# A four-layer graph network on one core: the instruction order as a stored table, and layer 0's tile turned through DRAM

## The chip, the core and the metric

The kernel runs on one core of a Trainium2 chip. The metric is device microseconds of one launch; the time before is the median of three runs. Engines go by their short names: PE (TensorE, the matrix engine), PEld (its weight loads), DVE (VectorE), ACT (ScalarE), POOL (GpSimd), SP (the queue that issues all the DMAs).

## What is computed

64 graphs of 256 nodes with 256 features go through four layers. Each is `x = x + layer(relu(layernorm(x)), adj)`:

```python
h = jnp.maximum(_layernorm(x, axis=-1), 0.0)
x = x + _L0_gnn_ref(h, adj, Wq, Wk, Wv, Wo, bo)   # masked attention, 8 heads of 32
h = jnp.maximum(_layernorm(x, axis=-1), 0.0)
x = x + _L1_gnn_ref(h, adj, W, a)                 # additive attention, softmax over axis 1, elu
h = jnp.maximum(_layernorm(x, axis=-1), 0.0)
x = x + _L2_gnn_ref(h, adj, weight, w_ih, w_hh, b_ih, b_hh)   # 3 rounds: A^T (h W_i), then a GRU cell
h = jnp.maximum(_layernorm(x, axis=-1), 0.0)
x = x + _L3_gnn_ref(h, adj, W, b, a)              # additive attention, 4 heads of 64
```

All of it is float32. In layer 0

```python
scores = jnp.where(adj > 0, q @ k.T / sqrt(32), -1e9)
w = softmax(scores)
out = (w @ v) @ Wo + bo
```

## The kernel before

**Tiling.** Two graphs make a pair; there are 32 pairs. A pair's x is one tile of 128 partitions by 1024 (four blocks of 128 nodes by 256 features). The loop over pairs at the end of the kernel does not issue anything: each step of each layer is given to `plan.add` with the engine or engines that may do it, its planned duration, what it reads and writes, and the buffers that it claims. The tile pool is by hand: `SLOTS` says how many buffers of each kind there are (22 of the large `w4`, 10 `part`, 6 `mask`, 8 banks of PSUM `ps`).

**Order.** `Plan.order` then places all 13630 steps one after the other. In before it is a list scheduler: of the steps whose inputs are placed and for which a buffer is free it takes the one that can begin first by its planned times. Ties are broken by a key: the pair's number times `PERIOD`, plus a number from `KEYS` for the stage (such as "0s", layer 0's scores) and the kind of engine, with a set of their own for the first pair ("<") and for the last two (">"). Where a step has two forms (`evict` at L380/L381 copies a PSUM bank out on ACT or on DVE; `either` goes to POOL or DVE) the scheduler chooses one. The buffer that a step gets is fixed there too. Each engine then executes its instructions strictly in the order so made, and SP issues all DMAs in its own. No time of the plan is measured; on the chip each engine waits for semaphores wherever its inputs are late.

**The start of a layer** is `norm_relu`. Statistics on DVE (L555, L557), the reciprocal root on POOL (L568, L569), then the scaled tile `xn` on ACT (L582) or DVE (L588). Matmuls need the features in partitions, so `xn` is turned. There are two ways. The one on PE: eight transposes of 128 by 128 into two PSUM banks (L627), and relu while copying out of PSUM on ACT or DVE (L639, L640). The other, `turn_rows`: DVE turns the 32 by 32 blocks of the tile (L731), one DMA writes the result to DRAM (L686) and four read it back with the blocks exchanged (L689); then relu goes from SBUF to SBUF. `by_dma` chooses: in before the second way is used for layer 2 (and for its state between its rounds, "2m", L718) in all pairs but the last. Layers 0 and 3 go by PE.

**Other lines of PE.** Layer 0: L786 q and k, L662 v, L807 scores (a mode that uses a quarter of the rows for each of four matmuls), L859 attention times v (a quarter of the columns), L874 the output product. Layer 1: L980, L994. Layer 2: L1064 messages, L1087 the GRU's gates. Layer 3: L1209, L1263 (half of the columns), and in the last pair alone L707, L1308. L1170 is layer 2's way back to rows in the last pair. L415, L437, L477 and L524 prepare weights once. Changing between full and partial use of the array is a mode switch.

**Other lines.** L697: DVE turns the blocks of attention weights, which then go through DRAM by L686 and L689 too. L755 adds mask and finds the minimum, L762 is exp with its sum, L839 divides a row on ACT or DVE, L1048/L1049 and L1099/L1097 are steps of layer 2 with a form on either engine, L1144 and L1184 are additions on DVE or POOL. L1117, L1135, L1150 and L1155 are the rest of the GRU on DVE.

Of the kernel before, what the change touches and what calls it, by code (L numbers as in the profile page):

```python
# [35 lines left out]
class Task:  # L36
    __slots__ = ("pair", "forms", "bufs", "rank", "stage", "mode", "before", "after", "waits", "begin", "end", "engine", "latency", "rest", "key", "index")


class Plan:  # L40

    HOP = {"PE": 0.22, "DVE": 0.15, "ACT": 0.17, "POOL": 0.2, "SP": 0.1}
    SAME = {"PE": 0.0, "DVE": 0.1, "ACT": 0.1, "POOL": 0.1, "SP": 0.0}  # L50

    SPARE, GRAIN = 2, 0.001
    SLOW, MARGIN = 1.4, 0
    BACK = {"DVE": 0.3, "POOL": 1.1}


    PERIOD = 2538  # L60


    KEYS = {
        ("io<", "SP"): -105537, ("w<", "SP"): 5780, ("w<", "on"): 21835, ("w<", "PE"): 92045, ("0n<", "on"): -17,
        ("0n<", "SP"): 6914, ("0n<", "PE"): -3050, ("0<", "on"): -27933, ("0<", "PE"): -18831,
        ("0s<", "PE"): -43638, ("0s<", "on"): 32209, ("0e<", "on"): 33228, ("0e<", "SP"): 79294,
        ("0c<", "PE"): -5710, ("0c<", "on"): 78141, ("1n<", "on"): -3936, ("1n<", "SP"): 18999, ("1<", "on"): 8087,
        ("1r<", "on"): -58751, ("1r<", "SP"): -50364, ("1e<", "on"): -20926, ("1c<", "PE"): -18939,
        ("1c<", "on"): -36902, ("2n<", "on"): -9735, ("2n<", "SP"): -46049, ("2<", "on"): 22518,
        ("2h<", "PE"): 10890, ("2h<", "on"): 963, ("2m<", "on"): -12912, ("2m<", "PE"): -339, ("2r<", "PE"): 6753,  # L70
        ("2r<", "on"): -6234, ("2z<", "PE"): 8380, ("2z<", "on"): -1814, ("2u<", "PE"): 8044, ("2u<", "on"): -10808,
        ("2b<", "on"): -14087, ("2b<", "SP"): 20724, ("3n<", "on"): -11783, ("3n<", "SP"): 82960,
        ("3n<", "PE"): -19591, ("3<", "on"): 17546, ("3<", "PE"): -92746, ("3r<", "on"): -497, ("3r<", "SP"): 37604,
        ("3e<", "on"): 40267, ("3e<", "SP"): 17882, ("3c<", "PE"): 7194, ("3c<", "on"): -53745,
        ("3b<", "on"): -23800, ("3b<", "SP"): -32005, ("out<", "SP"): -30439, ("io", "SP"): -97593,
        ("0n", "on"): -7813, ("0n", "SP"): 7384, ("0n", "PE"): -775, ("0", "on"): -21029, ("0", "PE"): -7985,
        ("0s", "PE"): -38312, ("0s", "on"): 31183, ("0e", "on"): 32073, ("0e", "SP"): 77616, ("0c", "PE"): 2974,
        ("0c", "on"): 57928, ("1n", "on"): -15346, ("1n", "SP"): 35194, ("1", "on"): 12385, ("1r", "on"): -77012,
        ("1r", "SP"): -49238, ("1e", "on"): -28359, ("1c", "PE"): -2261, ("1c", "on"): -48562, ("2n", "on"): -10735,
        ("2n", "SP"): -38216, ("2", "on"): 11427, ("2h", "PE"): 6520, ("2h", "on"): -16065, ("2m", "on"): -22340,  # L80
        ("2m", "PE"): 4183, ("2r", "PE"): 6841, ("2r", "on"): -20226, ("2z", "PE"): 8470, ("2z", "on"): 15796,
        ("2u", "PE"): 7640, ("2u", "on"): -22009, ("2b", "on"): -4038, ("2b", "SP"): 33111, ("3n", "on"): 144,
        ("3n", "SP"): 39097, ("3n", "PE"): -5812, ("3", "on"): 17370, ("3", "PE"): -71538, ("3r", "on"): 9250,
        ("3r", "SP"): 47648, ("3e", "on"): 7306, ("3e", "SP"): 29172, ("3c", "PE"): 14097, ("3c", "on"): -46777,
        ("3b", "on"): -25269, ("3b", "SP"): -31168, ("out", "SP"): -26306, ("io>", "SP"): -77815,
        ("0n>", "on"): -18200, ("0n>", "SP"): 5368, ("0n>", "PE"): -2327, ("0>", "on"): -9215, ("0>", "PE"): -23927,
        ("0s>", "PE"): -39218, ("0s>", "on"): 29982, ("0e>", "on"): 28489, ("0e>", "SP"): 110800,
        ("0c>", "PE"): 3058, ("0c>", "on"): 51808, ("1n>", "on"): -9527, ("1n>", "SP"): 16664, ("1>", "on"): -2988,
        ("1r>", "on"): -65640, ("1r>", "SP"): -57698, ("1e>", "on"): -21072, ("1c>", "PE"): -19804,
        ("1c>", "on"): -62098, ("2n>", "on"): -8753, ("2n>", "SP"): -47004, ("2>", "on"): 5930, ("2h>", "PE"): 1570,  # L90
        ("2h>", "on"): 2104, ("2m>", "on"): -12945, ("2m>", "PE"): 3645, ("2r>", "PE"): 7126, ("2r>", "on"): -31799,
        ("2z>", "PE"): 8512, ("2z>", "on"): -12839, ("2u>", "PE"): 7096, ("2u>", "on"): -20477, ("2b>", "on"): 2677,
        ("2b>", "SP"): 20159, ("3n>", "on"): -5070, ("3n>", "SP"): 60459, ("3n>", "PE"): -8408, ("3>", "on"): 8430,
        ("3>", "PE"): -69282, ("3r>", "on"): -4245, ("3r>", "SP"): 18290, ("3e>", "on"): 10463,
        ("3e>", "SP"): 23776, ("3c>", "PE"): 16211, ("3c>", "on"): -38642, ("3b>", "on"): -42787,
        ("3b>", "SP"): -42858, ("out>", "SP"): -18723, ("2n>", "PE"): 5512, ("2b>", "PE"): -10868,
        ("3e>", "PE"): -146212, ("3b>", "PE"): -24496,
    }


    SWITCH = 0.19
    HOLD = (0.00, 0.00, 0.00)
    MODES = ("full", "rows", "columns", "halves")

    def __init__(self, slots, spare):
        self.slots, self.spare = slots, spare
        self.pairs = []
        self.stage, self.rank, self.place = "", None, ""
# [4 lines left out]
    def add(self, forms, reads=(), writes=(), latency=0.0, claims=(), mode="full"):  # L113

        t = Task()  # L120
        t.pair, t.forms = len(self.pairs) - 1, [forms] if isinstance(forms, tuple) else forms
        t.before, t.after, t.bufs, t.latency = set(), [], [], latency
        t.end = t.engine = None
        t.rank = (t.pair if self.rank is None else self.rank, len(self.pairs[-1]))
        t.stage, t.mode = self.stage + self.place, mode
# [25 lines left out]
    def data(self, t, engine):  # L151

        return max(
            (x.end + (self.HOP[x.engine] if x.engine != engine else self.SAME[x.engine]) for x in t.before), default=0.0
        )

    def order(self):

        every = [t for tasks in self.pairs for t in tasks]
        spares = dict(self.spare, w4=self.SPARE)  # L160
        for i, t in enumerate(every):
            t.index, t.waits = i, len(t.before)
            for x in t.before:
                x.after.append(t)
            for b in t.bufs:
                b.until, b.left = 0.0, 0
                if not b.tag:
                    b.slot = 0
        for t in every:
            engine = t.forms[0][0]  # L170
            kind = engine if engine in ("PE", "SP") else "on"
            t.key = t.rank[0] * self.PERIOD + t.rank[1] * 1e-4 + self.KEYS.get((t.stage, kind), self.KEYS.get((t.stage.strip("<>"), kind), 0.0))
        for t in every:
            for b in t.bufs:
                b.left += 1
        free, now = {}, "full"
        slots = {tag: [(0.0, i) for i in range(n)] for tag, n in self.slots.items()}
        out = []
        left = [len(tasks) for tasks in self.pairs]
        ready = [t for t in every if not t.waits]  # L180
        oldest = 0
        while ready:
            best, fit, tiled = None, [], dict.fromkeys(self.MODES, 0)
            for t in ready:
                start = 0.0
                new = [b.tag for b in t.bufs if b.slot is None]
                for tag in set(new):
                    n = new.count(tag)
                    have = slots[tag]
                    if len(have) < n + (spares.get(tag, 0) if t.pair != oldest else 0):  # L190
                        break
                    start = max(start, have[n - 1][0])
                else:
                    fit.append((t, start))
                    if t.mode != "full" and max(start, self.data(t, "PE")) <= free.get("PE", 0.0) + 0.3:
                        tiled[t.mode] += 1
            for t, start in fit:
                for form in t.forms:
                    engine, key = form[0], t.key
                    data = max(start, self.data(t, engine))  # L200
                    begin = max(data, free.get(engine, 0.0), free.get("port", 0.0) if len(form) > 3 else 0.0)
                    at = begin
                    if engine == "PE":
                        if t.mode != now:
                            hold = self.HOLD[self.MODES.index(t.mode) - 1] if t.mode != "full" else 0.0
                            if hold and tiled[t.mode] < 2:
                                at = max(at, data + hold)
                            begin = max(at, free.get("PE", 0.0) + self.SWITCH)
                        elif t.mode != "full":
                            key -= 1e6  # L210
# [1172 lines left out]
```

## Time and profile before

| | |
|---|---|
| median of 3 runs | 3517.14 us (3517.03 to 3518.95) |
| the profiled execution | 3519.16 us |
| its span in the trace | 3517.4 us |
| granted clock of PE, mean | 0.993 |
| DMA | 720.92 MB, 64.9% of 16 engines' span in the main queue |

The rows of groups read: line, engine, operation, written tile <- read tiles, shapes, count | busy time in us, mean ns of one | idle time of the engine just before them, and what ended it.

```profile
L1087 PE MATMUL ps<-w,whhT 128*128 128x512 f32 x2304 | 1067.7, 593 | 1.5 <-DMA w<-turn 1.5
L627 PE MATMUL ps<-ident,w 128*128 128x128 f32 x520 | 70.9, 279 | 14.1 <-ACT w L582 14.0
L639 ACT ACTIVATE w<-ps 128x512 f32<-128x512 f32 x126 | 68.6, 599 | 84.6 <-PE ps L627 84.6
L731 DVE STREAM_TRANSPOSE w<-w 128x1024 f32<-128x1024 f32 x31 | 38.3, 1236 | 0.8 <-ACT w L582 0.8
L381 DVE COPY w<-ps 128x512 f32<-128x512 f32 x81 | 53.0, 682 | 11.7 <-PE ps L980 4.1 <-PE ps L1263 3.3 <-PE ps L1170 2.7
```

Mean durations of neighbours on one engine overlap, so a group's busy time is the union of its instructions' times. A float32 matmul of the program stands as two instructions in the trace, a transpose as one.

### The profile page before, as it was taken

The page shows a single profiled execution, that of the slowest core. Times are in us where ns is not written, and L with a number is a line of the kernel's source. Part 1 is how long each engine was busy: PE and PEld are TensorE (multiplying, and loading weights), DVE is VectorE, ACT ScalarE, POOL GpSimd, SP SyncE. Part 2 cuts the span into 40 slices and gives each one's busy share as a digit, 9 for nine tenths or more (in the row PEclk, how much of TensorE's full clock was granted, in tenths as well). Part 3 has the DMA queues.
Part 4 walks back from the last instruction along what each step waited for, and adds up shares of the span by engine and source line. Part 5 has one row for each costly group of instructions (what it writes and reads, how often), then busy time and mean ns, then how long its engine had stood idle before and what let it go on. Part 6 is the DMA issues. An engine that isn't in the chain of part 4 may idle for free.

```text
span 3517.4 us, 54023 instructions
## 1 busy us (share of the span) xinstructions
PE 3457.1 (98%) x15032; PEld 1944.5 (55%) x15032; DVE 2873.1 (82%) x8732; ACT 2674.8 (76%) x7097; POOL 347.9 (10%) x435
## 2 busy tenths in 40 slices
PE   9899999999999999999999999999999999999996
PEld 5455555555555555555555555555555555555553
DVE  6888987888988888978888878888878889887665
ACT  6776877877877877878877878878878778776545
POOL 2000110111001111001111001111001111001000
PEclk9999999999999999999999999999999999999998
DMA  6765677667667667667667666667666667666243
GB/s 195 216 190 179 213 225 222 204 213 231 211 203 220 211 204 239 205 205 219 212 203 234 207 209 218 210 208 234 204 210 215 211 215 232 202 217 191 96 138 126
DMA packets 573761, 720.92 MB, mean 205 GB/s; under 512 B 96532, under 2 KB 488724, under 8 KB 573460
## 3 DMA queue, kind: packets, MB, share of 16 engines
q1 hardware_dynamic: 573460, 717.46, 64.9%
q8 instruction: 121, 1.98, 0.2%
q14 instruction: 180, 1.47, 0.1%
HBM read 410.53 MB, written 298.34 MB: 202 GB/s over the span
## 4 chain that ended last, share of the span: by engine, by line
PE 90%; DVE 2%; ACT 1%; DMA 1%; issue 0%; SPq 0%; POOL 0%; DVEq 0%; ACTq 0%
PE ps L1087 54%; PE ps L1064 5%; PE ps L786 5%; PE ps L807 3%; PE ps L1209 3%; PE ps L1263 3%; PE ps L980 3%; PE ps L859 3%; PE ps L994 3%; PE ps L662 3%; PE ps L874 3%; PE ps L627 1%; DMA w<-turn 1%; DVE w L755 0%; ACT w L762 0%; DVE w L697 0%
## 5 line engine op out<-in xcount | busy, mean ns | idle before, releaser
L1087 PE MATMUL ps<-w,whhT 128*128 128x512 f32 x2304 | 1067.7, 593 | 1.5 <-DMA w<-turn 1.5
L1087 PE MATMUL ps<-w,giT 128*128 128x512 f32 x2304 | 1058.3, 592 | 0.7 <-ACT w L380 0.7
L762 ACT ACTIVATE w<-w,mx 128x256 f32<-128x256 f32 x1536 | 760.5, 504 | 7.5 <-DVE mx L755 7.4
L1087 PEld LDWEIGHTS ps<-w,giT 128*128 128x128 f32 x2304 | 436.8, 190 | 544.6 <-issue 527.9
L1087 PEld LDWEIGHTS ps<-w,whhT 128*128 128x128 f32 x2304 | 426.2, 190 | 467.5 <-issue 430.9
L380 ACT COPY w<-ps 128x512 f32<-128x512 f32 (+1 forms) x519 | 295.1, 580 | 290.7 <-PE ps L786 119.3
L697 DVE STREAM_TRANSPOSE w<-w 128x1024 f32<-128x1024 f32 x380 | 466.4, 1233 | 38.8 <-ACT w L839 28.2
L755 DVE CUSTOM_DVE_ANT_0 w<-ps,mask 128x256 f32<-128x256 f32 x1024 | 367.3, 416 | 21.0 <-PE ps L807 20.9
L839 ACT ACTIVATE w<-w,rz 128x256 f32<-128x256 f32 x782 | 341.9, 508 | 4.5 <-DVE rz L832 4.4
L762 ACT ACTIVATION_READ_ACCUMULATOR w<-w,mx 128x1 f32 x1536 | 301.2, 196 | 0.0
L1135 DVE TENSOR_TENSOR w<-ps,w 128x512 f32<-128x512 f32 x192 | 129.4, 674 | 209.1 <-PE ps L1087 208.5
L568 POOL TENSOR_SCALAR rs<-mv 128x4 f32<-128x4 f32 x129 | 32.5, 252 | 2703.1 <-DVE mv L557 2680.1
L582 ACT ACTIVATE w<-x,rs 128x256 f32<-128x256 f32 x492 | 257.4, 605 | 16.3 <-DVE rs L574 16.1
L1139 ACT ACTIVATE w<-w,bih_sb 128x512 f32<-128x512 f32 x192 | 138.4, 721 | 168.0 <-DVE w L1135 167.9
L1064 PE MATMUL ps<-part,part 128*128 128x256 f32 x1536 | 236.5, 303 | 5.3 <-DVE part L1022 4.3
L1240 ACT ACTIVATE w<-w,f 128x256 f32<-128x256 f32 x512 | 220.1, 498 | 5.5 <-DMA w<-row 5.4
L1112 ACT ACTIVATE w<-ps,brz 128x512 f32<-128x512 f32 x192 | 131.4, 685 | 121.8 <-PE ps L1087 121.7
L1064 PEld LDWEIGHTS ps<-part,part 128*128 128x128 f32 x1536 | 199.5, 190 | 41.2 <-issue 28.2
L755 DVE CUSTOM_DVE_ANT_0 w<-w,mask 128x256 f32<-128x256 f32 x512 | 195.4, 427 | 18.8 <-ACT w L1240 16.6
L1126 ACT ACTIVATE w<-ps,brz 128x512 f32<-128x512 f32 x192 | 131.8, 686 | 82.9 <-PE ps L1087 82.6
L555 DVE BATCH_NORM_STATS2 st<-x 128x6 f32<-128x256 f32 x512 | 188.8, 410 | 2.8 <-DMA x<-in_x_dram 2.3
L1117 DVE SCALAR_TENSOR_TENSOR w<-w,w 128x512 f32<-128x512 f32 x192 | 130.3, 679 | 60.5 <-ACT w L1112 58.0
(116 smaller groups left out, 4928.6 us busy)
## 6 DMA issues: line engine op xcount, KB each, us to landing
turn<-w SPq DMA_DIRECT2D x504, 512.0 KB
w<-turn SPq DMA_DIRECT2D x2016, 128.0 KB
w<-in_adj_dram SPq DMA_DIRECT2D x128, 512.0 KB
w<-row SPq DMA_DIRECT2D x64, 512.0 KB
x<-in_x_dram SPq DMA_DIRECT2D x64, 256.0 KB
out_dram<-x SPq DMA_DIRECT2D x64, 256.0 KB
turn<-w SPq DMA_DIRECT2D x62, 256.0 KB
w<-turn SPq DMA_DIRECT2D x248, 64.0 KB
```

The lines of the kernel that those rows point to most:

```text
L380: (A, act(n), lambda: nc.scalar.copy(dst(), src())),
L555: nc.vector.bn_stats(st()[:, t, :], tok(xt())[:, t, :])
L582: nc.scalar.activation(tok(xn())[:, t, :], tok(xt())[:, t, :], func, bias=rs()[:, 1, t : t + 1], scale=rs()[:, 0, t : t + 1])
L697: add((V, dve(T * N), lambda: nc.vector.transpose(blocks(), blocks())), writes=[e])
L755: nc.vector.tensor_tensor_reduce(row, src, mask, scale, 3.0e38, ALU.add, ALU.min, mn)
L762: nc.scalar.activation(row(e, r), row(e, r), AF.Exp, bias=mn()[:, r : r + 1], scale=-1.0, accum_out=zs()[:, z0(r) : z0(r) + 1])
L786: mm(ps(), w[:, k, o * P : (o + 1) * P], wide(hT, k), start=k == 0, stop=k == 1)
L839: op(row, row, rz()[:, r : r + 1])
L1064: mm(ps()[:, o * N : (o + 1) * N], chunk_of(part(), h.mixed, c, o), tok(ams[g](), N)[:, c, :], start=i == 0 and c == 0, stop=i == 1 and c ...
L1087: mm(ps(), w[:, k, c0 : c0 + P], wide(src, k), start=n == 0, stop=n == 2 * len(terms) - 1)
L1139: (A, act(N2, 1), lambda o=o, hn=hn: nc.scalar.activation(at_o(hn, o), at_o(hn, o), AF.Tanh, bias=bih_sb[:, 4 + o : 5 + o])),
L1240: nc.scalar.activation(dst, src, AF.Prelu, bias=f()[:, t, D + h : D + h + 1], alpha=ALPHA)
```

## The change

`Plan.order` no longer chooses. A table `ORDER` (a compressed byte string) holds three bytes for each step: the low and the high byte of a signed difference, and the number of the form. `ranked` adds the differences up within a pair to a rank, and the steps are sorted by it; `order` walks the sorted list, asserts that a step's inputs have been placed, and hands out buffers as before, by its planned times. The keys, the spare counts of the buffers and the ranks of the weights are gone. `SLOTS` has 21 `w4`, 11 `part` and 7 `mask`. `TURNED` has "0" too, so that layer 0's tile takes `turn_rows` in all pairs but the last. Every computed value is the same. New lines stand 37 below those of before (34 in the last part of the file): L627 is L664.

```diff
-    SPARE, GRAIN = 2, 0.001
-    SLOW, MARGIN = 1.4, 0
-    BACK = {"DVE": 0.3, "POOL": 1.1}
-    PERIOD = 2538
-    KEYS = {
...
-    }
+    SLOW, SWITCH = 1.4, 0.19
+
+    ORDER = (
...
+    )
+    def ranked(self):
+
+        every = [t for tasks in self.pairs for t in tasks]
+        n = len(every)
+        raw = zlib.decompress(base64.b85decode(self.ORDER))
+        assert len(raw) == 3 * n
+        low, high, forms = raw[:n], raw[n : 2 * n], raw[2 * n :]
+        rank, pair = 0, None
+        for t, a, b, form in zip(every, low, high, forms):
+            step = a + 256 * b
+            rank = (rank if t.pair == pair else 0) + (step - 65536 if step > 32767 else step)
+            pair = t.pair
+            t.rank, t.form = rank, t.forms[form]
+        return sorted(every, key=lambda t: t.rank)
...
-        while ready:
-            best, fit, tiled = None, [], dict.fromkeys(self.MODES, 0)
...
+        for t in every:
+            engine, us, do = t.form[:3]
+            assert t.before <= done
+            begin = max(free.get(engine, 0.0), free.get("port", 0.0) if len(t.form) > 3 else 0.0)
+            for x in t.before:
+                begin = max(begin, x.end + (self.HOP[x.engine] if x.engine != engine else self.SAME[engine]))
             for b in t.bufs:
                 if b.slot is None:
-                    _, b.slot = slots[b.tag].pop(0)
+                    at, b.slot = slots[b.tag].pop(0)
+                    begin = max(begin, at)
...
-        "w4": (22, [P, T * D], FP, 2),
-        "part": (10, [P, N2], FR, 1),
+        "w4": (21, [P, T * D], FP),
+        "part": (11, [P, N2], FR),
...
-        "mask": (6, [P, T * N], BF, 1),
+        "mask": (7, [P, T * N], BF),
...
-    TURNED = ("2", "2m")
+    TURNED = ("0", "2", "2m",)
...
-            for plan.rank, weights in ((None, weights0), (RANKS[0], weights1), (RANKS[1], weights2), (RANKS[2], weights3)):
+            for weights in (weights0, weights1, weights2, weights3):
                 weights()
```

## The prediction

> **What bounds the kernel now.** I read the busy shares first, then a table of the engines over seven stretches of the span, then the waits of TensorE, then the queue of TensorE in order of time, and last the groups by line and shape.
>
> ```profile
> PE 3457.1 (98%) x15032; PEld 1944.5 (55%) x15032; DVE 2873.1 (82%) x8732; ACT 2674.8 (76%) x7097; POOL 347.9 (10%) x435
> ```
>
> TensorE is busy for 3457.1 of 3517.4 us, so it idles 60.3 us; VectorE and ScalarE have 644 and 843 us free. The stretches (busy time of PE, PEld, DVE, ACT, POOL, then granted clock, DMA share, GB/s) tell where the 60 us lie:
>
> ```profile
> 0.00:110.00 110.00, 100.88 (x518) 64.39 (x519) 76.38 (x273) 75.20 (x207) 24.55 (x32) 1.00 0.65 208
> 110.00:250.00 140.00, 120.91 (x616) 72.16 (x615) 119.68 (x398) 110.47 (x316) 6.53 (x9) 0.94 0.70 210
> 250.00:500.00 250.00, 248.75 (x1054) 134.72 (x1053) 218.73 (x644) 180.38 (x481) 25.62 (x30) 1.00 0.62 194
> 500.00:3000.00 2500.00, 2500.00 (x10913) 1406.04 (x10911) 2077.93 (x6352) 1979.69 (x5258) 243.26 (x309) 1.00 0.68 215
> 3000.00:3400.00 400.00, 399.04 (x1610) 220.08 (x1609) 312.20 (x871) 266.61 (x674) 37.63 (x44) 1.00 0.54 170
> 3400.00:3460.00 60.00, 57.49 (x194) 29.39 (x192) 36.80 (x91) 27.33 (x61) 5.66 (x6) 1.00 0.39 123
> 3460.00:3518.00 58.00, 30.07 (x136) 17.75 (x136) 31.41 (x108) 35.09 (x105) 4.64 (x6) 0.71 0.43 137
> ```
>
> Idle TensorE: 9.1 us at the start, 19.1 us between 110 and 250, 2.2 us from 250 to 3400, 30.4 us behind 3400. From 500 to 3000 it has none, and no wait of TensorE is listed there. A busy row of matmuls is not yet a full TensorE, since their ends are modelled, so I look at starts: the queue of TensorE, start and length, shows each group beginning when the one before has issued its last.
>
> ```profile
> 1499.79 1.50 PE L1209 MATMUL ps<-w3a,w 128*128 128x264 f32 x6
> 1501.12 1.04 PE L627 MATMUL ps<-ident,w 128*128 128x128 f32 x8
> 1502.00 1.88 PE L1087 MATMUL ps<-w,whhT 128*128 128x512 f32 x4
> 1503.72 1.88 PE L1087 MATMUL ps<-w,giT 128*128 128x512 f32 x4
> 1505.43 3.60 PE L786 MATMUL ps<-w,wq_sb 128*128 128x512 f32 x8
> 1508.87 3.60 PE L786 MATMUL ps<-w,wk_sb 128*128 128x512 f32 x8
> ```
>
> Four matmuls of 512 columns take 1.72 us from start to start, every time: TensorE runs at its issue rate. The chain of waits repeats the same pieces every 106.02 us (one pair of graphs), and within such a period TensorE works 106.02 us, VectorE 88.20, ScalarE 84.22, GpSimd 10.22. So in the middle the only thing that shortens the kernel is fewer or cheaper instructions on TensorE; at the two ends it is fewer waits.
>
> **What the Trainium skill says.** "TensorE: Matmul & The Clock Gate", Part 4: PE-mode transpose, gives about 275 ns for one in context. Here the duration agrees (273 ns), but eight go from 1501.12 to 1502.00, so in a full queue one costs 0.11 us; I use that. The same page, Part 1, says that an idle window halves the clock until TensorE has been busy again: the trace agrees, 0.94 granted between 110 and 250 and 0.71 behind 3460, the two stretches with long waits. "VectorE: DVE Perf Modes", The three transpose paths: VectorE turns 32x32 blocks only, which is why the blocks must then be moved by DMA; the trace has this form at L731, 1236 ns for 128x1024. "SBUF — State Buffer", SBUF: two separate sides: GpSimd and certain VectorE operations lock a shared port pair from each other; no row here separates such blocking.
>
> **The change part by part** (line numbers of before; the counts of after are from the instruction order of the two programs).
>
> *Transposes of layer 0.* L627 falls from 520 to 272: 31 pairs by 8 leave. 248 x 0.109 (0.88 over 8) = 27.0 us off TensorE, and all on the bounding queue except the first few pairs. With them go 62 PSUM banks' worth of turns. Layer 0's tile now goes VectorE transpose (31 more of L731), one DMA to DRAM, four DMAs back, relu out of SBUF. This path is longer: in before the four reads are issued about 2.9 us after the write, when they follow at once (37.15 to 40.07), and the reads land some us later. That costs nothing while the pair starts early enough, and six buffers of x let its input be loaded ahead. It is not free for pair 0, where nothing lies ahead; there TensorE now starts with weight work before the first L786: 40 transposes at 0.11 and 36 of L477's 48 matmuls at 0.32 (three quarters of 0.43), 16 us. From the first start of TensorE in before (7.8 us, when the scaled tile is there) the turned tile needs 1.24 + 2.9 + the reads, for which I take 4, + 0.6 = 9 us, so the 16 us hide it.
>
> *Mode switches.* Counting changes between full, row, column and half use of the array in TensorE's order gives 364 before and 326 after. From the queue, a block of 16 at L807 holds it for 1.08 us (1521.34 to 1522.42), one of 64 at L859 for 3.59 (1515.83 to 1519.42): 0.052 each and 0.24 per block, 0.12 a switch. 38 x 0.12 = 4.6 us; I take 4.
>
> *Forms moved between engines.* VectorE gets 87 more copies out of PSUM (L381, 0.65), 28 of L588 (0.36), 104 of L839 (0.31), 52 of L1099 (0.74), 31 of L731 (1.24), 35 relus out of SBUF (no row before; between L1049's 0.43 and L640's 0.65, I take 0.6), and some 40 smaller (0.55), and loses 51 of L1144 (0.69) to GpSimd and about 10 of L1184: 57+10+32+38+38+21+22-35-6 = 177, less overlaps of neighbours about 165 us. VectorE goes to 2873+165 = 3038, 87% of 3483; in the middle 88.2+5.3 = 93.5 of 105.1 us. ScalarE loses roughly 87x0.58+28x0.52+104x0.44+52x0.67+43x0.6+20x0.6 = 183, to 71%. GpSimd gains 51x1.29+12x0.74 = 75, to 12%. All lie beside TensorE, and cost nothing while VectorE stays under it. Without that cover each us of VectorE beyond TensorE's in a period costs 1 us by 28 periods.
>
> *DMA and SP.* 155 more issues (31 writes at 0.34, 124 reads at 0.43) are 64 us on SP's queue, which is in order: a write that waits for L731 holds reads behind it, as the 476 us of L686 waiting for L697 do now without a wait of TensorE. Bytes: 31 x 1.02 MB = 32 MB on 720.9, share 64.9% to about 68%. Nothing in the middle waits for DMA now, so 0; if it did, up to 3 us a pair at a few pairs.
>
> *Buffers.* 21 for 22 of the large tiles while the turned path holds two more of them (its blocks and its turned copy); 11 for 10 and 7 for 6 of the small ones. The order is fixed with these counts, so a lack shows as waits, counted below.
>
> *The order itself.* Start: the waits of 110 to 250 plus the half clock there, (1-0.94) x 140 = 8.4, make 27.5 us. A search over whole orders can fill these, and can also open others: between 0 and -27; I take -8, under a third, since pair 0's input now comes later. Middle: before is exactly periodic (every 264 TensorE instructions of the listing); after is not for most of the first half. TensorE's queue is in order, so any instruction put too early stops it. Between 0 and, if every period had one late eviction of about 2 us, +56; I take +5, because VectorE, the engine it depends on most, still has 11 us free in a period. The tail: the last turns are L1170, L627, L1209, L1263, L707 as before, a chain of one pair with nothing beside it, still by TensorE in the last pair: 0.
>
> Sum: -27 -4 -8 +5 = -34. The profiled execution took 3519.16 (span 3517.4 and 1.8 around it), so 3485; the median of the runs shown is 2 us lower, 3517.14, so **3483 us**.
>
> **Rivals.**
> *Slower: VectorE late by a little in each period.* For it: 93.5 of 105.1 us, the listing gives single periods some 5% above that, and L1135 (196 us in the middle) is already where VectorE and TensorE hand over. Against: now VectorE waits for TensorE, not the reverse. Price: 1.6 us at 28 periods = 45 us, -31+45 = +14: 3531. It decides from 31+7 = 38 us, 1.4 us a period, where it passes 0.2%.
> *Given back at the ends.* The first q and k wait for the DRAM path and the pipeline fills later; 31 us more of waits there: 3517. Against: the 16 us of weight work ahead.
> *More than forecast.* Start waits and half clock all filled: -31-27 = 3459. For it: those were the only movable waits. Against: they are chains of layers 1 and 2 of the first pair.
>
> **How the numbers follow.** Forecast 0.62, spread 3468 to 3505; more 0.17 (3450 to 3468); given back 0.07; slower 0.14. A measurement tells 0.2%, 7 us, from no change. Faster than 3510: 0.79; within: 0.07; slower than 3524: 0.14. The range 3458 to 3512 leaves out the slower case (0.14) and the lowest part of the larger gain (0.06).
>
> **What would show it.** L627's successor has 272 transposes; TensorE's busy time falls to about 3425; the middle still has under 10 us idle and a period of about 105 us; VectorE stands near 87%, ScalarE near 71%, DMA near 68%. Wrong would be: waits of TensorE for VectorE or for turned tiles in the middle (VectorE late), a clock under 1.00 there, or more than 40 us idle before 250.

## The result and the profile after

The changed kernel took 3499.66 us (median of 6 runs, 3497.33 to 3508.78) beside 3517.66 us of the kernel before (6 runs, 3515.85 to 3518.98): a ratio of 0.9954, 95% interval 0.9941 to 0.9967 (the ratio goes by the means of the runs, 16 us apart; the medians are 18 us apart). The forecast was 3483. The direction was right, and about half of the gain came: 16 to 18 us of 34. The profiled execution took 3501.53 us, with a span of 3499.7.

The busy shares of after (engine, busy us, share of the span, instructions):

```profile
PE 3433.5 (98%) x14784; PEld 1931.6 (55%) x14784; DVE 3078.1 (88%) x9047; ACT 2522.0 (72%) x6739; POOL 453.1 (13%) x497
```

The engine shares are within two points of those forecast. TensorE has 248 instructions fewer, yet its busy time fell by 23.6 us only, and 66.2 us of the span stand beside it, where before had 60.3. The same stretches as before, of after:

```profile
0.00:110.00 110.00, 94.25 (x484) 59.21 (x484) 92.89 (x324) 80.93 (x240) 20.11 (x29) 0.98 0.86 281
110.00:250.00 140.00, 130.33 (x567) 79.03 (x568) 108.86 (x327) 91.20 (x237) 13.10 (x15) 0.95 0.56 164
250.00:500.00 250.00, 246.87 (x1152) 138.08 (x1151) 226.42 (x675) 187.65 (x519) 30.36 (x34) 1.00 0.69 216
500.00:3000.00 2500.00, 2486.22 (x10738) 1393.81 (x10737) 2262.69 (x6641) 1861.53 (x4970) 343.89 (x367) 1.00 0.73 225
3000.00:3400.00 400.00, 397.13 (x1542) 218.12 (x1541) 318.55 (x882) 252.62 (x647) 39.77 (x44) 1.00 0.56 172
3400.00:3460.00 60.00, 53.38 (x183) 27.77 (x181) 40.62 (x98) 29.91 (x77) 3.61 (x6) 0.94 0.46 144
3460.00:3500.00 40.00, 25.37 (x125) 15.52 (x124) 28.10 (x107) 18.17 (x55) 2.22 (x3) 0.76 0.52 161
```

The stretch from 500 to 3000, where TensorE of before never idled, now has 13.8 us of visible idle time; under 10 was forecast. Cut finer, again of after:

```profile
250.00:1000.00 750.00, 739.54 (x3239) 412.89 (x3237) 679.14 (x1984) 546.58 (x1478) 105.83 (x116) 1.00 0.71 220
1000.00:2000.00 1000.00, 994.30 (x4326) 557.23 (x4325) 905.05 (x2677) 739.20 (x1991) 138.23 (x146) 1.00 0.73 225
2000.00:3000.00 1000.00, 999.24 (x4327) 561.77 (x4326) 904.92 (x2655) 763.41 (x2022) 130.19 (x139) 1.00 0.73 226
```

Read the second and third line against each other: VectorE works 905 us in both and the DMA share is 0.73 in both, but TensorE idles 5.7 us in the one and 0.8 in the other. What differs is the order. In the table of after, pairs 21 and 22 have one and the same order, 424 places apart, and so do 402 of the 424 steps of pair 23. Towards both sides this fades: at pairs 18 and 26 some 200 steps still stand 424 places behind those of the pair before, at pairs 2 to 16 at most 42. I call the stretch from 2000 to 3000 the periodic one and that from 250 to 2000 the irregular one. The groups by line and shape, of after:

```profile
L1124 PE MATMUL ps<-w,whhT 128*128 128x512 f32 x2304 | 1071.2, 594 | 1.2 <-DVE mx L792 1.0
L768 DVE STREAM_TRANSPOSE w<-w 128x1024 f32<-128x1024 f32 x62 | 76.7, 1238 | 17.3 <-ACT w L619 11.6 <-PE ps L1124 5.2
L664 PE MATMUL ps<-ident,w 128*128 128x128 f32 x272 | 39.1, 280 | 8.1 <-DVE w L625 5.8 <-ACT w L619 2.3
L676 ACT ACTIVATE w<-ps 128x512 f32<-128x512 f32 x31 | 17.4, 586 | 15.3 <-PE ps L664 15.3
```

The transposes are down to 272, and VectorE's turns of whole tiles up to 62. What TensorE waits for, of after (line waited for, us in total, times, longest):

```profile
PE ps L896 <- DMA w<-turn: 12.8, 4, 8.4
PE ps L452 <- DMA w<-in_L_gnn_w_ih_dram: 6.9, 1, 6.9
PE ps L664 <- DVE w L625: 5.8, 2, 3.5
PE ps L1246 <- ACT w L676: 3.8, 4, 2.2
PE ps L844 <- ACT w L417: 2.9, 3, 2.1
```

The list goes on with some 28 entries of 0.2 to 2.7 us, spread over many lines of TensorE and over ScalarE, VectorE and the DMA as releasers: there is no one late transfer or engine. How such a wait arises shows in the order of time (start, length, engine, operation; in brackets the idle time ahead), of after around 1917:

```profile
1914.67 1.04 PE L664 MATMUL ps<-ident,w 128*128 128x128 f32 x8
...
1915.54 1.88 PE L1124 MATMUL ps<-w,giT 128*128 128x512 f32 x4
...
1916.14 0.69 DVE L1181 TENSOR_TENSOR w<-w,w 128x512 f32<-128x512 f32 x1
...
1916.86 0.69 DVE L1187 SCALAR_TENSOR_TENSOR w<-w,w 128x512 f32<-128x512 f32 x1
...
1917.47 0.22 DVE L997 RECIPROCAL rz<-zs 128x2 f32<-128x2 f32 x2
1917.67 0.91 ACT L1000 ACTIVATE w<-w,rz 128x256 f32<-128x256 f32 x2 [0.49 <-DVE rz L997]
...
1918.48 1.06 ACT L676 ACTIVATE w<-ps 128x512 f32<-128x512 f32 x2
...
1919.59 0.49 PE L1246 MATMUL ps<-w3a,w 128*128 128x264 f32 x1 [2.17 <-ACT w L676]
```

The transposes of layer 3 (L664) are done at 1915.7. Their relu (L676) stands on ScalarE behind four exponentials (L994, left out here) and L1000, which waits for two reciprocals (L997, 0.22 us), and these stand on VectorE behind two steps of layer 2 of 0.69 us. So the relu starts 2.8 us after its input was there, and TensorE, with one group of 1.72 us put between, runs dry for 2.17 us. ScalarE idled only 0.49 us of the 2.8; the rest it spent on work that the table puts ahead of the relu. Each queue runs in its order, and this order leaves TensorE no time to spare here. (The Trainium skill, "TensorE: Matmul & The Clock Gate", in the table at its head, calls the queues of ScalarE and VectorE strictly first in, first out; this trace agrees.)

**A ledger.** Idle time in the listing is not all that is lost, since the ends of matmuls are modelled. I therefore count each TensorE instruction by its start and give it the step from start to start that it has in a full queue: 0.429 us for one of 512 columns, 0.2155 for 256, 0.2225 for 264, 0.120 for 256 in the faster type (L1101), 0.109 for a transpose, 0.0533 for a row or column tile, and so on. The sum is the work of a stretch; what the stretch takes above it is "over". (It contains the mode switches, so it is never 0.)

| us over the work | 0–250 | 250–1000 | 1000–2000 | 2000–3000 | 3000–3400 | 3400–end | work, all | over, all |
|---|---|---|---|---|---|---|---|---|
| before | 53.8 | 20.2 | 21.5 | 20.8 | 7.0 | 44.8 | 3349.4 | 168.0 |
| after | 47.4 | 33.7 | 31.4 | 21.1 | 9.3 | 34.4 | 3322.4 | 177.4 |
| difference | -6.4 | +13.5 | +9.9 | +0.3 | +2.3 | -10.4 | -27.0 | +9.4 |

That the work fell by 27.0 us is the count of 248 transposes times the 0.109 us of the prediction, since the ledger uses the same price; the listing above shows that the price still holds, with eight transposes from 1914.67 to 1915.54. -27.0 + 9.4 is, but for rounding, the 17.7 us by which the span fell. So the missing gain went into 250 to 2000: 23.4 us. A second trace of the same kernel (after_again, below), counted the same way, moves by up to 3 us in a stretch (about 44 at the start, 37 and 29 in the next two), while its sum from 250 to 2000 stays (about 66 for 65.1); differences of 3 us in one stretch are not read as an effect.

Only 15 us of the 23.4 stand there as idle time (16.2 for 1.3). Two pieces of 3.4 us at half the clock, one at 558 after a wait of 2.97 us and one at 1920 after the wait shown above, cost half of their length, 3.4 us together: in the second the instructions of 264 columns go 0.440 us from start to start, for 0.222 beside it. The remaining 5 us do not show as idle time.

### The profile page after: what moved, and what is told of

Read it like the earlier page. It is cut to its first block, busy times and chain, and to the rows that moved or that the text cites. A ratio compares the mean times of both kernels' runs of the same rounds, so it can differ in the third digit from the quotient of the medians.

```text
span 3499.7 us, 53732 instructions
## 1 busy us (share of the span) xinstructions
PE 3433.5 (98%) x14784; PEld 1931.6 (55%) x14784; DVE 3078.1 (88%) x9047; ACT 2522.0 (72%) x6739; POOL 453.1 (13%) x497
## 3 DMA queue, kind: packets, MB, share of 16 engines
q1 hardware_dynamic: 595780, 749.98, 69.3%
## 4 chain that ended last, share of the span: by engine, by line
PE 64%; DVE 7%; DMA 3%; ACT 2%; issue 1%; SPq 1%; POOL 0%; DVEq 0%; ACTq 0%; POOLq 0%
PE ps L1124 37%; PE ps L823 4%; PE ps L1101 4%; PE ps L1246 3%; PE ps L844 3%; PE ps L1300 2%; PE ps L699 2%; PE ps L1031 2%; PE ps L896 2%; PE ps L1017 2%; PE ps L911 2%; DMA w<-turn 2%; DVE w L792 1%; DVE w L954 1%; DVE x L1334 1%
## 5 line engine op out<-in xcount | busy, mean ns | idle before, releaser
L799 ACT ACTIVATE w<-w,mx 128x256 f32<-128x256 f32 x1536 | 759.2, 499 | 45.2 <-DVE mx L792 43.7
L417 ACT COPY w<-ps 128x512 f32<-128x512 f32 x431 | 244.2, 579 | 198.1 <-PE ps L1300 79.0
L876 ACT ACTIVATE w<-w,rz 128x256 f32<-128x256 f32 x678 | 292.4, 498 | 88.4 <-DVE rz L869 85.1
L619 ACT ACTIVATE w<-x,rs 128x256 f32<-128x256 f32 x464 | 244.7, 591 | 93.3 <-DVE rs L611 88.9
L799 ACT ACTIVATION_READ_ACCUMULATOR w<-w,mx 128x1 f32 x1536 | 293.4, 191 | 0.0
L1181 POOL TENSOR_TENSOR w<-w,w 128x512 f32<-128x512 f32 x86 | 114.0, 1332 | 1147.9 <-PE ps L1124 368.4
L1101 PE MATMUL ps<-part,part 128*128 128x256 f32 x1536 | 228.8, 299 | 1.8 <-DVE part L1091 1.7
L605 POOL TENSOR_SCALAR rs<-mv 128x4 f32<-128x4 f32 x129 | 40.9, 317 | 1368.0 <-DVE mv L594 1301.1
L1101 PEld LDWEIGHTS ps<-part,part 128*128 128x128 f32 x1536 | 197.3, 190 | 32.1 <-issue 18.3
L792 DVE CUSTOM_DVE_ANT_0 w<-w,mask 128x256 f32<-128x256 f32 x512 | 196.4, 428 | 13.3 <-ACT w L1277 12.4
```

Of the source, the lines that this page charges most:

```text
L417: (A, act(n), lambda: nc.scalar.copy(dst(), src())),
L619: nc.scalar.activation(tok(xn())[:, t, :], tok(xt())[:, t, :], func, bias=rs()[:, 1, t : t + 1], scale=rs()[:, 0, t : t + 1])
L792: nc.vector.tensor_tensor_reduce(row, src, mask, scale, 3.0e38, ALU.add, ALU.min, mn)
L799: nc.scalar.activation(row(e, r), row(e, r), AF.Exp, bias=mn()[:, r : r + 1], scale=-1.0, accum_out=zs()[:, z0(r) : z0(r) + 1])
L876: op(row, row, rz()[:, r : r + 1])
L1101: mm(ps()[:, o * N : (o + 1) * N], chunk_of(part(), h.mixed, c, o), tok(ams[g](), N)[:, c, :], start=i == 0 and c == 0, stop=i == 1 and c ...
```

## The experiments

The theory formed from this: the order of the table is too tight between 250 and 2000, so small delays on any engine reach TensorE. The rivals: VectorE's load at 88% (my own slower case), the DMA's load, and the path through DRAM itself. All ratios are to the kernel before on the same chip, with 95% intervals.

### The two halves of the change

The turn of layer 0 through DRAM alone, with the scheduler of before (and the buffer counts of after):

```diff
-        "w4": (22, [P, T * D], FP, 2),
-        "part": (10, [P, N2], FR, 1),
+        "w4": (21, [P, T * D], FP, 2),
+        "part": (11, [P, N2], FR, 1),
...
-        "mask": (6, [P, T * N], BF, 1),
+        "mask": (7, [P, T * N], BF, 1),
...
-    TURNED = ("2", "2m")
+    TURNED = ("0", "2", "2m")
```

> The scheduler of before kept, with layer 0 turned by VectorE and DRAM in all pairs but the last and with the buffer counts of after (21, 11, 7); no table. Theory of placement (the 26 us that the middle lost lie at single steps which the table puts too early in an engine's order, in the stretch where no two pairs are ordered alike): a periodic middle without waits, so the 27 us of transposes are gained in full, start and tail as before or a few us later: 3486 to 3496 us. Theory of load (VectorE at 90% in the middle makes copies late): VectorE stands at about 85% here, so the result is the same as for placement. Theory of transfers (the longer way through DRAM is what comes late): waits of TensorE for turned tiles in the middle, 3500 or more.

Measured: 3706.07 us (3699.61 to 3708.26), ratio 1.0527 (1.0513 to 1.0542). The work is the 3322.4 us of after, but 384 us lie over it, more than before's in every stretch, and 186.9 us of the span run at half clock. Only the theory of transfers (3500 or more) left room for such a time; the 3486 to 3496 of the others failed. TensorE's waits are spread over many lines, and turned tiles have a part in them: L1087 waits 32.6 us in all for those of layer 2, as the largest group, 17.5 of them before 250. Keys searched anew for it were not tried, and the buffer counts changed too, so the run shows that the turn needed another order than these keys give, and not more.

The table alone: the table of after with layer 0 turned by TensorE, each transpose placed just ahead of its relu's place.

```diff
-    TURNED = ("0", "2", "2m",)
+    TURNED = ("2", "2m")
...
+        for a, c, first, rank in later:
+            for r in range(rank, first, -1):
+                if sum(lo <= r and hi >= r - 0.5 for lo, hi in spans) < self.slots["ps"]:
+                    break
...
+            a.rank, c.rank = r - 0.5, r - 0.25
```

> The table's order kept, but layer 0's tile turned by TensorE in all pairs, as before: its transposes stand just ahead of the places of the relus. Placement: the table's waits stay and the 27 us come back: 3522 to 3530 us, slower than before. Load: VectorE has 38 us less, the middle loses some of its waits: 3510 to 3518. Transfers: 32 MB and 155 DMAs less, the waits on turned tiles go too: 3505 to 3515.

Measured: 3534.70 us (3532.81 to 3542.66), ratio 1.0049 (1.0037 to 1.0062). Over the work: 40.5 to 250, 37.6 to 1000, 38.4 to 2000, 27.0 to 3000, 10.2 to 3400, 34.3 behind. Two things follow. The shorter tail (34.3 and 34.4 against 44.8) belongs to the table. And the start is 13.3 us better than before's by the table, of which the turn gives 6.9 back (47.4; about 4 by the second trace of after). The time lies above the 3522 to 3530 expected if the waits stay and the 27 us come back, and well above what the theories of load and transfers expected. The middle loses here too, although nothing of layer 0 goes through DRAM and VectorE stands at 86%: the turned path is not needed for such a loss. But the transposes were squeezed into an order made without them, which adds to it by an amount that this run cannot separate.

### Is it the load of an engine?

From pair 3 to 27, 207 steps of VectorE that ScalarE can do too go to ScalarE; and, in another kernel, every third such step of ScalarE (156) goes to VectorE. Places in the order stay.

```diff
+        for tasks in self.pairs[3:28]:
+            for t in tasks:
+                if len(t.forms) == 2 and t.forms[0][0] == "ACT" and t.form[0] == "DVE" and len(t.form) == 3:
+                    t.form = t.forms[0]
```

> As after, but in pairs 3 to 27 all 207 steps that read and write one tile and may go on ScalarE or VectorE, and that the table gives to VectorE, go to ScalarE; places in the order unchanged. VectorE falls from 88% to about 84%, ScalarE rises to about 75%. Load: most of the middle's 20 us of waits go, 3480 to 3487 us. Placement: no gain, other steps are late on ScalarE instead: 3495 to 3515. Transfers: no change.

> As after, but in pairs 3 to 27 every third of the steps that the table gives to ScalarE and that could go to VectorE goes to VectorE (156 of them), places unchanged. VectorE rises by about 95 us to 91%, 93% in the middle. Load: waits of TensorE in the middle at least double, also in the periodic stretch from 2000 to 3000: 3515 us or more. Placement: a few more late steps, 3500 to 3512, the periodic stretch still nearly without waits. Transfers: no change.

Measured: 3531.75 us (3530.92 to 3537.04), ratio 1.0040 (1.0026 to 1.0054), with less on VectorE; and 3542.86 (3537.10 to 3544.40), ratio 1.0064 (1.0050 to 1.0078), with more. Relieving VectorE did not help: taking work off it (88% down to 84%) cost 32 us beside after, putting work on it (90%) 43. The first lies above every range expected (load 3480 to 3487, placement 3495 to 3515). The second has the number of load (3515 or more), not of placement (3500 to 3512), but not the sign of load, waits at least doubled in the periodic stretch too: TensorE idles 1.4 us there, for 0.8. From 1000 to 2000 both have 50 us over the work (after 31.4), while from 2000 to 3000 they have 26.0 and 23.5 (after 21.1). A change of load in either direction harms the irregular stretch and costs the periodic one 2 to 5 us. That speaks against VectorE's load, and for an order in which every place counts.

The same dose on before, every third such step of ScalarE (214) to VectorE:

```diff
+            if 3 <= t.pair < 28 and len(t.forms) == 2 and engine == "ACT" and t.forms[1][0] == "DVE" and len(t.forms[1]) == 3:
+                count = self.count = getattr(self, "count", 0) + 1
+                if count % 3 == 0:
+                    do = t.forms[1][2]
```

> The kernel before, its order untouched, but in pairs 3 to 27 every third of the steps on ScalarE that could go to VectorE goes there (214 of them, about 125 us; 85% of the span). The same kind of dose cost the table 43 us with 156 steps. Fragile order: within 10 us of before. Load (VectorE's share decides): at 85%, below after's 88%, also no loss, so a loss of over 15 us would speak against both and for a price of any disturbed order.

Measured: 3534.62 us (3533.71 to 3535.42), ratio 1.0045 (1.0031 to 1.0058): 15 us, spread evenly, about 5 us per 1000 (23.5, 26.5, 25.8 over the work). More steps moved than in the dose on after (214 for 156), and a third of its loss. It is still more than the 10 us expected of an order with room, and at the 15 us that were to speak for a price of any disturbed order; and VectorE ends at 86% here, for 90% there, so this pair of runs does not part order from load.

DMA: two more copies of 512 KB from DRAM to DRAM per pair, of the input `adj` into a tile that nothing reads, in after and in before. The output is unchanged.

```diff
+    sinks = [dram.tile([P, T * N], I32, name=f"sink_{i}") for i in range(8)]
...
+                for i in range(2):
+                    nc.sync.dma_start(
+                        tok(sinks[(2 * p + i) % 8], N), adj[2 * p : 2 * p + 2].rearrange("g (c p) d -> p (g c) d", p=P))
```

> As after, with two more copies of 512 KB per pair from the adjacency matrix to scratch in DRAM, issued behind layer 0's load of it: as many bytes again as layer 0's turn brought in, output unchanged. Transfers: the waits on turned tiles and with them the time rise by 10 us or more. Placement and load: within 5 us of after, since in the periodic stretch nothing waits for DMA.

> The kernel before with the same two extra copies of 512 KB per pair that cost the table 36 us. Theory of a fragile order (what the table lost in the middle is slack: steps stand so close behind what they need that any lateness reaches TensorE, while the scheduler's periodic order has room): within 8 us of before, no waits of TensorE between 500 and 3000. Theory of transfers (DMA time itself decides in both): 20 us or more slower, waits of TensorE for turned tiles in the middle.

Measured: after with the dose 3536.12 us (3533.30 to 3541.15), ratio 1.0049 (1.0036 to 1.0062), 36 us more than without; before with the dose 3529.06 (3524.61 to 3534.87), ratio 1.0031 (1.0019 to 1.0042), 10 us more. The 36 us are what the theory of transfers expected (10 or more), not that of placement (within 5); the 10 us lie just beyond the 8 of a fragile order and far below the 20 of transfers. In the trace of before with the dose only the start pays (62.0 for 53.8), and the stretch from 1000 to 3000 has no wait at all. That trace is of the fastest of its runs, 3524.61, so where the slower ones lose is not shown. The stretches 500 to 3000 of before with the dose:

```profile
500.00:3000.00 2500.00, 2500.00 (x10913) 1406.38 (x10912) 2085.45 (x6367) 1984.83 (x5276) 243.05 (x309) 1.00 0.73 225
```

Here the DMA share is 0.73 and the rate 225 GB/s, just what after has in the same stretch, and TensorE does not wait. The bytes as such are not the cause of a wait. In after the dose costs 12.9 us at the start, 14.8 from 250 to 1000, 6.4 to 2000 and nothing (-0.2) from 2000 to 3000.

After itself, unchanged, in one of these sessions:

> The changed kernel as it is, to have it on the same chip and in the same rounds as the runs beside it: 3497 to 3509 us. If the four changed tables so far were slower because of the chip and not of their changes, this one is near 3530 too.

Measured: 3499.66 us (3497.77 to 3504.87), ratio 0.9948 (0.9935 to 0.9960). The waits come back where they were: 3.31 us at 555.4 (L896, as the 2.97 at 558.6), 2.81 at 970.5 (L1031, as the 1.02 at 972.0), 2.16 at 1918.5 (L1246, as the 2.17 above). Their places belong to the order, not to the run; their lengths can differ.

### The periodic order sooner

If the periodic order has no waits, let it begin sooner: pairs 14 to 20 take places and forms of pair 22, 424 places apart.

```diff
+        for p in range(14, 21):
+            for t, m in zip(self.pairs[p], self.pairs[22]):
+                t.rank, t.form = m.rank + (p - 22) * 424, t.forms[m.forms.index(m.form)]
```

> As after, but pairs 14 to 20 take the order and the forms of pair 22, moved by 424 places a pair; everything else is the table's. Placement: TensorE no longer idles between about 1400 and 2000 us, where after has 5.7 us of idle time and one stretch at half clock; total 3490 to 3495 us. Load: VectorE's load is the same, no change, 3497 to 3502. Transfers: no change.

Measured: 3528.17 us (9 runs, 3523.90 to 3534.38), ratio 1.0028 (1.0018 to 1.0037). The gain did not come; the expectation of it failed. From 1000 to 2000 the time over the work is 58.8 us, all the long waits of that stretch lie between 1318 and 1773, around where the orders of pairs 13 and 14 meet, and none follow until 3000.

The same from pair 6 on, with 6 of 13630 steps moved so that the buffers suffice:

> As after, but pairs 6 to 20 all take the order and forms of pair 22, and 6 of 13630 steps move a little so that buffers suffice. In the run with pairs 14 to 20 TensorE waited only where the old and the new stretch meet. Fragile order: a joint of some 25 us between about 450 and 950 in the place of after's 13 us there, then no waits up to 3000, 10 us saved between 1000 and 2000: 3495 to 3515 us. Load or transfers: waits all through as in after, 3497 to 3502.

Measured: 3530.61 us (3529.65 to 3533.10), ratio 1.0034 (1.0021 to 1.0046), no gain either, and outside the 3495 to 3515 expected: the joint costs 44 us more than after has there, for the 12 expected. But the stretches of this kernel tell the two things apart:

```profile
250.00:1000.00 750.00, 712.56 (x3042) 394.80 (x3041) 641.90 (x1885) 522.39 (x1418) 96.42 (x105) 0.98 0.67 209
1000.00:2000.00 1000.00, 1000.00 (x4365) 562.63 (x4364) 906.89 (x2659) 769.46 (x2041) 125.21 (x131) 1.00 0.73 226
2000.00:3000.00 1000.00, 999.46 (x4317) 558.94 (x4316) 909.10 (x2680) 764.85 (x2036) 126.20 (x138) 1.00 0.72 225
```

From 1000 to 2000 TensorE is full, with VectorE at 906.89 us and the DMA at 0.73: the loads of after, without its waits (19.8 us over the work for 31.4). The joint from 250 to 1000 has 77.4 for 33.7. So the loads allow a full TensorE in that stretch, and a sudden change of order costs more than the irregular table.

### An order with slack

The last two runs test the theory. A local search starts from the table of after and moves steps a few places or changes their form; it reckons with lengths taken from the trace of after and takes every hand-over between engines 0.2 to 0.35 us longer and DMAs up to twice as long as planned, so that a step stands behind what it needs by that much in the plan. The steps and the computation are the same, and so are the buffer counts. Half of the steps then stand 13 places or more from where they stood, and 711 of 13630 take another form.

```diff
     ORDER = (
-        "c-rlI2Y_T%m3Ezb?|b*<S2=f8=iJki6U>kqh9FVNf`bxFxW-*vcSZDHRM1_+qO7>AxQa?rRz*hQNQMbaf?;y%?&;}R)m{1B{}wPamAa>TNTS"
...
+        "c-qZ-2Yg)BmHwQ2@9S;mO>de}@70pKjcr_Tz@da*lMqS>B-tdJu)8S`0tpErZ8ssCkdQyAkkAPbI+$jRF<@M<!A&lbWy#V=n*Q$pY5{wi<T2PG`bnPA=#~3U`Of#9a}BhuOR8Dl_U"
...
```

> The kernel after with another table: same steps, same computation, TURNED with layer 0, same SLOTS. The table comes from a local search that starts from the table of after, but reckons with lengths taken from the trace of after (start to start of neighbours in a full queue: VectorE's turn 1.16, its four-part sum into x 0.78, a prelu on ScalarE 0.40) and asks for slack: every hand-over between engines is taken 0.2 to 0.35 us longer and every DMA up to twice as long as the plan has it, so that a step of TensorE stands behind what it needs by that much. Theory (the middle of after loses because its irregular stretch stands too close behind what it needs): with slack the whole stretch from 250 to 3000 has next to no visible wait, what stands over the issue time of TensorE's instructions there falls from after's 86 us to about what before has in its stretch without waits, 17 to 21 us per 1000, so 50 to 57; start and tail as in after or a little better. 3322 + 48 + 55 + 9 + 34 = 3468; 3455 to 3475. Rival (the loss is the engines' load itself, VectorE at 88% and the DMA at 69%, whatever the order): waits stay or move, time 3495 to 3510 as after.

The second kernel is searched in the same way with layer 0 turned by TensorE:

```diff
-    TURNED = ("0", "2", "2m",)
+    TURNED = ("2", "2m")
```

> The same search with the same slack, but layer 0's tile turned by TensorE (TURNED without layer 0, 248 transposes more), started from the table of table_pe; same SLOTS as after, same computation. If the order is what limited both, the two searched tables differ by what the DRAM turn is worth alone: the 27.0 us of transposes, less the 7 that its start was seen to cost, so this one stands 17 to 27 us above margins, at about 3480 to 3500, and also beats before. Rival (the turn through DRAM is worth nothing once a good order hides or removes the waits, or the margin search only helped the lighter load on VectorE): the two stand within 7 us of each other, or this one is the faster.

Measured: with the turn through DRAM 3467.28 us (3467.08 to 3469.12), ratio 0.9851 (0.9837 to 0.9864); with TensorE's turn 3484.71 (3484.02 to 3488.16), ratio 0.9901 (0.9888 to 0.9915). Both beat before and after, and both stand where the theory put them (3468 was expected of the first, 17 to 27 more of the second, and 17 came). Busy shares and stretches of the first:

```profile
PE 3421.2 (99%) x14784; PEld 1918.3 (55%) x14784; DVE 3089.3 (89%) x9144; ACT 2468.5 (71%) x6622; POOL 469.5 (14%) x505
```

```profile
110.00:250.00 140.00, 137.02 (x640) 80.82 (x633) 114.89 (x329) 86.50 (x223) 14.52 (x16) 0.98 0.57 171
250.00:500.00 250.00, 248.39 (x1102) 136.30 (x1101) 229.74 (x692) 190.99 (x537) 32.24 (x36) 1.00 0.69 216
500.00:3000.00 2500.00, 2498.06 (x10800) 1397.43 (x10799) 2281.12 (x6709) 1827.19 (x4889) 365.49 (x381) 1.00 0.74 226
3000.00:3400.00 400.00, 399.59 (x1586) 221.23 (x1585) 317.90 (x893) 242.37 (x615) 34.26 (x39) 1.00 0.56 172
```

VectorE works more than in after (89% for 88%, and 2281 for 2263 us from 500 to 3000) and the DMA as much, and TensorE idles 1.9 us there where after idled 13.8. Nor is this order periodic: in its table at most 25 of a pair's 424 steps stand one common number of places behind those of the pair before, in the stretch from 2000 to 3000 too. So an irregular order as such does not make TensorE wait.

| us over the work | 0–250 | 250–1000 | 1000–2000 | 2000–3000 | 3000–3400 | 3400–end | work, all | over, all |
|---|---|---|---|---|---|---|---|---|
| after | 47.4 | 33.7 | 31.4 | 21.1 | 9.3 | 34.4 | 3322.4 | 177.4 |
| slack, turn through DRAM | 38.9 | 20.4 | 23.3 | 20.3 | 7.1 | 34.3 | 3322.4 | 144.3 |
| slack, turn by TensorE | 31.5 | 19.0 | 21.0 | 21.0 | 5.9 | 34.5 | 3349.4 | 132.8 |

From 250 to 2000 the loss is back: 65.1 us become 43.7, and before has 41.7. A further 8.5 us come from the start. The parts were not all as expected: 64.0 us over the work from 250 to 3000 where 50 to 57 were written, and 38.9 at the start for 48. So most of the 23 us were a property of this table, and not of the turn or of a load. The two searched kernels, whose spans are 15.6 us apart, also give the price of the turn, as far as one searched order for each can tell: 27.0 us of work saved, 7.4 paid at the start (38.9 against 31.5), 4.1 in the rest, which is little more than two traces of one kernel differ by.

What stays open: the search had the measured lengths and the slack together, and was one more search besides, so the runs do not say which of these did more; no trace measures the slack of the hand-overs itself. How the table of after was searched is not in the file. And no run shows why a joint of two orders costs as much as it does.

## Where the prediction was right, and where it failed

**Transposes, -27.0.** Right: L664 stands with 272, and eight still take 0.87 us of TensorE's queue. The shares of engines (VectorE 87% forecast, 88% found; ScalarE 71 and 72; GpSimd 12 and 13; DMA 68 and 69.3) came close too, and the forms moved the way that was read, but the sizes were rougher than the shares tell: VectorE gained 205 us for 165, ScalarE lost 153 for 183, GpSimd gained 105 for 75.

**Mode switches, -4.** The count is right (364 and 326), the size cannot be read alone. It is not what decides: the kernel with slack has 355 switches and is 32 us faster than after with 326.

**Start, -8.** Measured -6.4 up to 250. The sum was near, in part by luck: the table brought 13.3 and the turn took 6.9 back (about 4 by the second trace), which I had put at nothing, hidden under 16 us of weight work. For the first q and k the hiding held: L823 starts at 28.45 us after a wait of 0.9 us, and in table_pe, where TensorE turns, at 28.58. The two largest waits of the start, 6.9 us of L452 for a load and 8.4 of L896 at 116 for turned attention weights, are not the turn's, since table_pe has them too (7.7 and 7.9). What the turn cost is small pieces: the scores of layer 0 (L844) wait 4.4 us in after and 1.2 in table_pe; the rest is not traced to lines.

**Middle, +5.** This is the step that failed. Over the work, 250 to 2000 gave +23.4, and 2000 to 3400 +2.6; with the 4 us that fewer switches should have taken off in it, the term is about +30, where +5 stood. I had named the right danger, one late hand-over at a time in a queue that runs in order, and had seen that the order of after is not periodic for most of the first half. But I sized it by VectorE's free time in a period (11 us), and that is not what sets it: with VectorE as full or fuller, the periodic stretch, the periodic order from pair 6 (from 1000 on) and the order with slack have next to no waits. Free time is a mean over a period. That what counts instead is how far ahead of TensorE each single result is ready is what the waits in the listings and the last two runs point to; its share beside the measured lengths stays open.

**Tail, 0.** Measured -10.4, by the table, since table_pe has it too. I had taken the chain of the last pair as fixed because its lines are the same. Its waits are not: behind 3400, L707 waited 9.9 us for exponentials (L762) in before and its successor L744 0.8 in after, and L1170 waited 6.6 us for VectorE, its successor L1207 2.7.

The two misses partly cancel: the forecast of -34 with 1.6 less at the start, about 25 more in the middle and 10.4 less at the tail gives the -17.7 of the span.

Of the rivals, "VectorE late by a little in each period" did not happen: the waits came mainly in the irregular stretch, not in each period, and moving work off VectorE made it worse. "Given back at the ends" is refuted by both ends, which gained. "More than forecast" did not come with this table either; the start and the tail gained 16.8 us together, and the middle took more than that.

## What to carry to other kernels

Before a fixed order replaces one that runs in a steady period, ask how much earlier than needed each result is ready, and not only how busy the engine is that makes it: engine loads did not tell the late order from the full one here. A search over orders should use lengths measured in the trace and demand slack at each hand-over; here the two together were worth 32 us, where the change itself brought 18. And when a change comes with a new order, search an order for the old variant as well, or the order's loss or gain is booked to the change (here: 17 us between two searched orders).

## What the runs showed of the hardware

- Waits hide in busy time. TensorE stands at 98% in before and in after, while the time over the work went from 168.0 to 177.4 us. The Trainium skill, "Perfetto Trace Analysis", Identifying the Most-Contended Engine, says that matmul busy time is not a good measure, and this case agrees. Of the two measures that it offers instead, the share of weight loads did not help here: 55% in before, after and the kernel with slack, which is 52 us faster than before. The start-to-start ledger told them apart.
- Half-clock pieces in the middle are 3.4 us long or a multiple of it. In after a wait of 2.97 us and one of 2.17 (at 1919.6) each had one behind them, in the kernel with slack one of 1.61 us had none. The wait at 1918.5 of the second trace of after, at the same place of the order and 2.16 us long, had none. The two do not always go together: in the kernel with the periodic order from pair 14 a wait of 2.54 us at 560 had none, and one of 1.12 at 1318 had one. "TensorE: Matmul & The Clock Gate", What's actually happening, has an idle window of about 3.4 us that runs freely; the unit agrees, and that the same wait has a piece in one execution and none in another fits a window that runs freely; but here such pieces follow waits shorter than it.
- The runs of after spread wider than those of before: 3497.33 to 3508.78 beside 3515.85 to 3518.98. The kernel with slack spreads over 2 us, 3467.08 to 3469.12. That a tight order also makes the time less steady is suggested by this, and not shown.
